# Layer 2 FFN's first slots inside layer 2 attention's tail, one sequence's roots on VectorE, and constant products in layer 0's FFN

## The chip, the cores and the metric

The kernel runs on one core of a Trainium2 chip. The core has five engines that run on their own and meet at semaphores: TensorE (PE: matrix products and transposes; its weight loads are listed as PEld), VectorE (DVE), ScalarE (ACT), GpSimd (POOL) and SyncE (SP, which here only issues DMAs). The metric is the device time of one execution in microseconds; the time before is the median of three, 2713.35 us (2712.96 to 2721.79).

## The reference

Four layers, each FFN, attention, FFN around a residual `x` of 4 sequences x 512 positions x 128 features in float32:

```python
x = x + 0.5 * ffn(layernorm(x));  x = x + attn(layernorm(x));  x = x + 0.5 * ffn(layernorm(x))
```

Two of the FFNs matter here. Layer 0's FFN takes the mean over the positions of a GELU of 1024 input patterns, keeps for each sequence the 128 largest, passes them to 512 process patterns, keeps the 64 largest, weighs 64-wide values by their softmax, passes the sum to 1024 output patterns and keeps the 128 largest of these; the result is one row that is added to all positions of its sequence. So between its wide first products and its last sum, all work is on vectors of a few hundred to a thousand numbers for each sequence.

Layer 2's FFN is a mixture of 8 experts: a router (128 x 8) chooses one expert for each position, and that expert's gated network (128 to 2 x 512, `a * sigmoid(g)`, 512 to 128) is applied to it, with its biases and unscaled. Layer 2's attention, between the two calls of this FFN, attends inside blocks of 32 positions, 16 heads of 8.

## The kernel before

Everything stays in the core's own memory, `x` and the normed copy `y` as 16 tiles of 128 positions (four tiles a sequence), `yT` as features x positions. Python loops unroll the whole program. A scheduler orders each engine's instructions by a planner's costs; what is passed to `tc.keep_in_program_order` (`mm_in_order` L174, `transpose_in_order`, `pin`) keeps the order of the Python text on its engine, everything else may be placed where it is ready. `mm` (L168) and `transpose` are not so held.

**Small work between the big steps.** `chain(b)` collects small steps of sequence `b` (statistics, scaling, transposes, router logits, routing); `tick()` is called many times in each attention loop and runs the steps whose gap of ticks has passed. `leave_normed` puts into such a chain: statistics of `x`, scaling into `y`, `turn` (transposes into `yT`), and, if the next stage routes, `logits`, and after an odd sequence the three parts of `route`: `choose` (softmax over 8 and first maximum), `count` (positions within each expert, the slots' experts `ei`) and `find` (which position goes to which place in which slot, `come`).

**A root.** `inverse_root` (L189) makes `1/sqrt(v + eps)` for a few numbers a partition: a VectorE addition (L197) and a power on POOL (L198). `statistics` (L212) calls it for four tiles. For wider inputs it uses a bit trick and two Newton steps, eight instructions. `scaled_by_act` (L244) then makes `-mean * r` with two POOL instructions and scales on ACT.

**Layer 0's FFN** (`l0_ffn`, run twice). After the wide products, `largest` finds the 128 largest of 1024: 16 rounds of `max` (8 numbers) and `match_replace` on VectorE (L401, L403), a tree of merges (L409), one transpose `pt_l` of the limit (TensorE), comparisons and prefix sums on VectorE, and two products `place` with constant matrices that number the ties. Then come `pp4` (8 products of 512 columns), `pp`, eight rounds of `max` for the 64 largest (L466), softmax, `pt_w`, `pg`, `po0`, `largest` once more, `po1` and `pb`, which spreads the result to all partitions for the update of `x` (L506). The second call is followed by layer 1's FFN, whose attention begins with products of a constant matrix whose result nobody reads (`idle_product`, L179).

**Layer 2's FFN** (`l2_ffn`, run twice, before and after layer 2's attention). The 2048 positions go in two passes of 8 tiles (sequences 0 and 1, then 2 and 3). In a pass the positions are sorted by expert into at most 15 slots of 128 rows, each slot for one expert (`PASS` = 8, `SLOTS` = 15). `logits` has stored the rows in HBM (`yd`). `slot_steps` makes a queue of steps; step n does

- `send(n-2)`: stores a finished slot `o` to `od` in HBM (SP),
- `load(n+5)`: reads the slot's expert from `ei` and loads that expert's weights, 836 KB, into one of five `w` buffers (SP, L1352),
- `fetch(n+4)`: gathers the slot's 128 rows `xg` from HBM (POOL, L1356),
- `to_features(n+1)`: one transpose, copied out by ACT as `xT`,
- `hidden(n)`: 8 products of 128 columns into the banks `pg` and `pa`, four sigmoids on ACT (L1374), four products `hT` on VectorE (L1375),
- `result(n-1)`: 4 products into `po2`, and the bias on VectorE (L1384).

A buffer of `w` comes free when `result` of its slot has added the bias out of it. The second pass begins after the first (`fetch_result` then gathers the first pass's results back from `od`, L1402). In `l2_ffn` the first pass's steps are spread by hand between what is left of the last sequence's chain: `between` says how many steps follow when so many parts of that chain are left.

**Layer 2's attention** (`l2_attn`). A loop over n = -9 to 19, five places in each; tile n's scores are in step n, its exponentials in n+1, the transposes of the weights (`pt_2a`) in n+2, its sums with the values (`po_2a`) in n+3; a sequence's output is made in step 4b+7 (`turn_sums`, `output`). So from n = 16 on nothing new begins. The chain of sequence 1 reaches `find` at n = 14, and the first pass could be routed from there; its first load and gather are in `l2_ffn`, after the loop.

Of the kernel before, what the change touches and what calls it, by code (L numbers as in the profile page):

```python
# [40 lines left out]
PASS = NT // 2  # L41
SLOTS = PASS + 7


# [60 lines left out]
def tile_macaron(ctx, tc, x_in, const_in, vec_in, w0_in, ws_in, ws3_in, w2f_in, w3_in, out):  # L105
# [73 lines left out]
    def idle_product(tag, n):  # L179

        mm_in_order(bank(tag, "idle")[:, :n], onesm, cst[:, :n])

    def bcast(ap, n):

        return ap[:, :, None].to_broadcast([ap.shape[0], ap.shape[1], n])
# [4 lines left out]

    def inverse_root(sb, dst, src, name, op, c, eng=None):


        n = src.shape[-1]
        if n <= TB:
            v = sb.tile([P, n], F32, tag=name, name=name, bufs=2)
            (eng or nc.vector).tensor_scalar(v, src, c, None, op)  # L197
            nc.gpsimd.tensor_tensor(dst, v, minus_half[:, :n], ALU.pow)  # L198
            return
# [5 lines left out]
        for to, a, b in ((yy, -0.703952253, 1.681913895), (dst, -0.50000016, 1.50000048)):  # L205
# [4 lines left out]
            else:  # L210
                eng.tensor_mul(t, t, xx)
                eng.tensor_scalar(t, t, a, b, ALU.mult, ALU.add)  # L212
                eng.tensor_mul(to, t, yy)

    def statistics(src, b, eng=None, pinned=False):

        st = keep.tile([P, TB, 6], F32, tag="ln_st", name="ln_st", bufs=2)
        mv = keep.tile([P, TB, 2], F32, tag="ln_mv", name="ln_mv", bufs=3)
        r = keep.tile([P, TB], F32, tag="ln_r", name="ln_r", bufs=3)
        for t in range(TB):  # L220
            first = nc.vector.bn_stats(st[:, t, :], src[:, b * TB + t, :])
            if pinned and t == 0:
                tc.keep_in_program_order(first)
            nc.vector.bn_aggr(mv[:, t, :], st[:, t, :])
        inverse_root(keep, r, mv[:, :, 1], "ir4", ALU.add, 1e-5, eng)
        return mv, r
# [10 lines left out]

    ordered = {"act": False}

# [4 lines left out]
    def scaled_by_act(dst, src, b, stats):  # L244

        mv, r = stats
        m = keep.tile([P, TB], F32, tag="ln_m", name="ln_m", bufs=3)
        nc.gpsimd.tensor_mul(m, mv[:, :, 0], r)
        nc.gpsimd.tensor_scalar_mul(m, m, -1.0)
        for i in range(TB):  # L250
# [106 lines left out]
    def l0_ffn(tag, chained):  # L357
        with pool(tag) as sb:
# [18 lines left out]
            def by_neuron(row, name):  # L377
# [3 lines left out]
                for c in range(2):  # L381
                    transpose(pt[:, ts(c, P)], row[:, ts(c, P)])
                nc.vector.tensor_copy(
# [11 lines left out]
            def largest(row, vals, r):  # L395
# [3 lines left out]
                for i in range(P // 8):  # L399
                    m8, src = order[:, ts(i, 8)], w if i else row  # L400
                    nc.vector.max(m8, src)  # L401
                    if i < P // 8 - 1:
                        nc.vector.match_replace(w, m8, src, GONE)  # L403
                two = [sb.tile([64, P], F32, tag=f"two{i}", name="two") for i in range(2)]
                larger(two[0], order, 64, 64)
# [9 lines left out]
                pt = bank("t", "pt_l")  # L415
                transpose(pt[:, :B], turned)
                lim = sb.tile([P, B], F32, tag="lim", name="lim")
# [15 lines left out]
                flat = lambda v: v.rearrange("p c b -> p (c b)")  # L433
                mm(place[:, : 8 * B], const("m1"), flat(equal), True, False)
                mm(place[:, : 8 * B], ones, flat(sums[1]), False, True)
                nc.vector.scalar_tensor_tensor(
# [6 lines left out]
            for c in range(2):  # L443
                transpose(pt[:, ts(c, P)], acc[:, c, :, :].rearrange("p q b -> p (q b)"))
            nc.vector.tensor_scalar_mul(ra, pt[:, :256], 1.0 / S)
# [6 lines left out]
            for c in range(8):  # L452
                mm(p4[ts(c % 4, 32), :], kept[0][:, c, :], piw[:, c, :], c < 4, c >= 4)
            pq = sb.tile([P, 512], F32, name="pq4")
            nc.vector.tensor_copy(pq[:, 0:256], p4[:, 0:256])
            nc.vector.tensor_copy(pq[:, 256:512], p4[:, 256:512])
            pp = bank("m", "pp")
            mm(pp[:B, :], selb.rearrange("p (b n) -> p b n", n=P)[:, :, 0], pq)
            pa = sb.tile([B, 512], F32, name="pact")
# [4 lines left out]
            for i in range(KP // 8):  # L464
# [3 lines left out]
                if i == 0:  # L468
                    nc.vector.tensor_scalar_mul(nm, m8[:, 0:1], -1.0)
            ea = sb.tile([B, 512], F32, name="ea")  # L470
            nc.scalar.activation(ea, pa, AF.Exp, bias=nm)
# [6 lines left out]
            for c in range(4):  # L478
                transpose(pt[:, ts(c, B)], pw[:, ts(c, P)])
            pwT = sb.tile([P, 4, B], F32, name="pwT")  # L480
# [3 lines left out]
            for c in range(4):  # L484
                mm(pg[:64, :B], pv[:, c, :], pwT[:, c, :], c == 0, c == 3)
            nc.vector.tensor_copy(agg[:, :B], pg[:64, :B])
# [3 lines left out]
            for q in range(4):  # L490
                mm(po[ts(q, 32), :256], agg, oiw[:64, ts(q, 256)])
            nc.scalar.activation(oa, po[:, :256], AF.Gelu)
# [3 lines left out]
            for c in range(8):  # L496
                mm(po[ts(c % 4, 32), :D], kept[1][:, c, :], op[:, c, :], c < 4, c >= 4)
            o4 = sb.tile([P, D], F32, name="o4")
            nc.vector.tensor_copy(o4, po[:, :D])
            pb = bank("m", "pb")  # L500
            for b in range(B):
                mm(pb[:, ts(b, D)], selb[:, ts(b, P)], o4)

# [748 lines left out]
    yds = [dram.tile([P * PASS, D], F32, name=f"yd{i}") for i in range(2)]  # L1252
    routed, passes = {}, {}

# [11 lines left out]
    def route(k):  # L1266
# [22 lines left out]
        def count():  # L1289
# [13 lines left out]
            nc.vector.tensor_reduce(base, tri, AX.X, ALU.add)  # L1303
            nc.vector.tensor_add(end, base, nf)
            to = sb.tile([P, PASS, 8], F32, tag="to", name="to")
            nc.vector.scalar_tensor_tensor(
# [16 lines left out]
            for t in range(PASS):  # L1323
                nc.vector.tensor_scalar(st["in_place"][:, t, :], const("iota"), place[:, t : t + 1], None, ALU.is_equal)
            past = sb.tile([P, SLOTS, 8], F32, tag="past", name="past")
            nc.vector.tensor_tensor(past, bcast(const("iota")[:, :SLOTS], 8), rows(end, SLOTS), ALU.is_ge)
            es = sb.tile([P, SLOTS], F32, tag="es", name="es")
            nc.vector.tensor_reduce(es, past, AX.X, ALU.add)
            ei = st["ei"] = sb.tile([P, SLOTS], I32, tag=f"ei{k}", name="ei")
            nc.vector.tensor_scalar_min(ei, es, 7.0)  # L1330

# [9 lines left out]

    def slot_steps(sb, k, tags):

        st, yd = passes[k], yds[k]
        ei, come = st["ei"], st["come"]
# [3 lines left out]
        def load(s):  # L1349
            e = nc.values_load(ei[0:1, s : s + 1], engines=[mybir.EngineType.SP], min_val=0, max_val=7)  # L1350
            w[s] = sb.tile([P, W2F.n], F32, tag="w", name="w", bufs=5)
            nc.sync.dma_start(w[s], w2f_in[bass.ds(e, 1), :, :].rearrange("e p n -> (e p) n"))  # L1352

        def fetch(s):
            xg = sb.tile([P, D], F32, tag="xg", name="xg", bufs=4)
            nc.gpsimd.indirect_dma_start(xg, None, yd[:, :], bass.IndirectOffsetOnAxis(ap=come[:, s : s + 1], axis=0))  # L1356
            xT[s] = xg

        def to_features(s):
            pt = bank(tags["t"], "pt_x")  # L1360
            transpose_in_order(pt[:, :P], xT[s])
            xT[s] = sb.tile([P, P], F32, tag="xT", name="xT", bufs=3)
            nc.scalar.copy(xT[s], pt[:, :P])

        def hidden(s):
            pg, pa = bank(tags["g"], "pg2"), bank(tags["a"], "pa2")
            w1, b1 = W2F(w[s], "w1"), W2F(w[s], "b1")
            for half, p in ((1, pg), (0, pa)):
                for c in range(4):
                    mm_in_order(p[:, ts(c, P)], w1[:, ts(4 * half + c, P)], xT[s])  # L1370
            hT[s] = sb.tile([P, 4, P], F32, tag="hT", name="hT", bufs=3)
            for c in range(4):
                sg = sb.tile([P, P], F32, tag="sg", name="sg", bufs=4)
                nc.scalar.activation(sg, pg[:, ts(c, P)], AF.Sigmoid, bias=b1[:, 4 + c : 5 + c])  # L1374
# [3 lines left out]
        def result(s):  # L1378
            po = bank(tags["m"], "po2")
            w2 = W2F(w[s], "w2")  # L1380
            for c in range(4):
                mm_in_order(po[:, :D], hT[s][:, c, :], w2[:, ts(c, D)], c == 0, c == 3)
            o = sb.tile([P, D], F32, tag="o", name="o", bufs=4)
            nc.vector.tensor_add(o, po[:, :D], W2F(w[s], "b2"))  # L1384
# [6 lines left out]
        def step(n):  # L1391
            for part, lag in ((send, 2), (load, -5), (fetch, -4), (to_features, -1), (hidden, 0), (result, 1)):
                if 0 <= n - lag < SLOTS:
                    part(n - lag)

        return deque(lambda n=n: step(n) for n in range(-5, SLOTS + 3))

# [17 lines left out]

    def l2_ffn(tag, early, between, ticks, gap):

        ready.clear()
        own = {"g": "g", "a": "a", "t": "t", "m": "m"}
        with pool(tag) as sb:  # L1420
            with banks(tag + "pa", **early):
                tags = {"g": "e", "a": "e", "t": "m", "m": "m"} if "e" in early else own
                steps = None
                while chains:
# [44 lines left out]

    def l2_attn(v4s):  # L1470
        pin = tc.keep_in_program_order
        with pool("l2a") as sb:
# [128 lines left out]
            for n in range(-9, NT + 4):  # L1601
                for place, (part, lag) in enumerate(stages):
# [6 lines left out]
                    if n >= 0 or place == 0:  # L1609
                        tick()  # L1610


# [362 lines left out]
    with pool("ws") as wp:  # L1975
# [9 lines left out]
        with pool("l2x") as l2x:  # L1985
            with pool("l1x") as xb:
# [8 lines left out]
                l2_ffn("l2f", {"e": 6, "m": 2}, {23: 3, 19: 2, 10: 4, 2: 3, 1: 3}, (5, 8), 4)  # L1995
            with banks("ps2"):
                routed |= {"g": l2x.tile([P, NT, 8], F32, tag="g2f", name="g2f"), "sb": l2x, "gap": 4}
                l2_attn(v4s)
            l2_ffn("l2g", {"a": 2, "g": 2, "t": 2, "m": 2}, {5: 2, 2: 3, 1: 3}, (19, 31), 10)
    with pool("l3r") as rb:  # L2000
# [148 lines left out]
```

## Time and profile before

| | us |
|---|---|
| median of three executions | 2713.35 |
| the profiled execution | 2706.51 |
| its span, first to last instruction | 2704.8 |
| TensorE busy | 2222.7 (82%) |
| VectorE busy | 1780.4 (66%) |
| ScalarE busy | 1293.6 (48%) |
| GpSimd busy | 959.3 (35%) |
| mean granted clock of TensorE | 0.894 |
| layer 0 FFN, narrow part, first and second call | 50 to 125, 308 to 382 |
| layer 1 FFN's last sequence and layer 2 FFN, first call | about 1160 to 1310 |
| layer 2 attention's tail | 1414 to 1440 |
| layer 2 FFN, second call: first pass, second pass | 1440 to 1500, 1500 to 1551 |

The clock is the share of full speed that the chip grants to TensorE: in this trace it is 1.0 or 0.5, and the means over a stretch lie between. A line of a timeline gives the start, the duration, engine, line, operation, output `<-` inputs, shapes and count, and in brackets how long the engine was idle before it and what ended that.

### The profile page before, as it was taken

To read this page: it belongs to the slowest core of one execution; us is meant where nothing else is said; L and a number is where in the kernel's file an instruction comes from. 1 tells how busy PE (TensorE), PEld (TensorE's weight loads), DVE (VectorE), ACT (ScalarE), POOL (GpSimd) and SP (SyncE) were. 2 spreads that over 40 slices of the span, in tenths; PEclk is the share of its full clock that TensorE was granted. 3 is DMA by queue.
4 is the path that set the end of the run, shared out by engine and by line. 5 is a ranking of instruction groups with operands and counts; after the bars stand their busy time and mean duration, and the time that the engine had idled before them with its cause. 6 is when DMAs were issued, how large, how long until landed. Compare 5 with 4: busy or idle time off the path is not lost. (4 is left out here: it accounts for less than half of the span.)

```text
span 2704.8 us, 50539 instructions
## 1 busy us (share of the span) xinstructions
PE 2222.7 (82%) x18934; PEld 1260.1 (47%) x18934; DVE 1780.4 (66%) x4768; ACT 1293.6 (48%) x3145; POOL 959.3 (35%) x1540
## 2 busy tenths in 40 slices
PE   4277539989778998979767868998889999789988
PEld 2145214434334443458557845555533333455555
DVE  3645376777556777555674477778567775877774
ACT  3044314444423544334333447776525555677774
POOL 2013012333222322334322377676310000877661
PEclk8579759998779999889877989999989999899998
DMA  3043010000000000037205811100000000110100
GB/s 144 0 156 96 0 63 1 1 1 1 1 1 1 2 1 5 5 119 246 100 9 191 266 33 23 22 20 21 5 1 1 1 1 5 28 23 21 23 20 12
DMA packets 38412, 113.17 MB, mean 42 GB/s; under 512 B 6872, under 2 KB 14808, under 8 KB 37656
## 3 DMA queue, kind: packets, MB, share of 16 engines
q1 hardware_dynamic: 34792, 100.94, 11.7%
q0 software_dynamic: 2944, 6.04, 1.3%
q8 instruction: 149, 2.44, 0.4%
q10 hardware_dynamic: 432, 2.98, 0.3%
q14 instruction: 95, 0.78, 0.1%
HBM read 79.78 MB, written 15.47 MB: 35 GB/s over the span
## 5 line engine op out<-in xcount | busy, mean ns | idle before, releaser
L845 ACT ACTIVATE PT<-pk_at 128x512 f32<-128x512 f32 (+3 forms) x768 | 335.4, 488 | 401.6 <-PE pq_at L174 255.7
L174 PE MATMUL pk_at<-qx,km 32*128 32x512 f32 (+3 forms) x1536 | 400.8, 555 | 5.8 <-ACT PT L845 2.7
L817 DVE CUSTOM_DVE_ANT_0 s<-pq_at,cst 128x384 f32<-128x384 f32 (+3 forms) x512 | 249.8, 488 | 98.6 <-PE pq_at L174 45.6
L174 PE MATMUL pq_at<-km,qT 32*128 32x128 f32 (+3 forms) x1024 | 277.2, 505 | 19.1 <-DVE nm L817 15.1
L1678 ACT ACTIVATE s<-s,nm,rn 128x128 f32<-128x128 f32 x512 | 245.5, 482 | 3.1 <-DVE nm L1790 2.3
L848 POOL TENSOR_SCALAR_AFFINE_SELECT PT<-PT 128x256 f32<-128x256 f32 x256 | 104.8, 411 | 387.6 <-ACT PT L845 387.6
L174 PEld LDWEIGHTS pk_at<-qx,km 32*128 32x128 f32 x1536 | 147.0, 190 | 153.4 <-issue 92.4
L174 PE MATMUL po_at<-PT,vh 128*32 128x128 f32 (+3 forms) x2432 | 203.6, 392 | 5.1 <-POOL PT L848 5.0
L819 DVE TENSOR_REDUCE nm<-pq_at 128x1 f32<-128x512 f32 x256 | 165.4, 685 | 55.3 <-PE pq_at L174 53.8
L198 POOL TENSOR_TENSOR ln_r<-ir,minus_half 128x4 f32<-128x4 f32 x64 | 66.1, 1035 | 359.6 <-DVE ir L197 358.4
L1739 POOL TENSOR_TENSOR t<-t,t 128x1024 f32<-128x1024 f32 x64 | 151.7, 2370 | 111.5 <-DVE t L1735 111.2
L174 PE MATMUL pq_at<-km,t 32*128 32x512 f32 x512 | 170.8, 661 | 0.7 <-DVE nm L819 0.4
L174 PE MATMUL p_qk<-w,hT 128*128 128x512 f32 x256 | 136.6, 659 | 10.1 <-DVE t L1735 8.7
L1802 POOL TENSOR_TENSOR s<-s,sm 128x1024 f32<-128x1024 f32 x64 | 121.4, 1897 | 51.1 <-DVE sm L1801 43.1
L171 PE MATMUL pt<-ident,s 128*128 128x128 f32 x640 | 92.2, 291 | 51.9 <-POOL s L1802 34.9
L174 PEld LDWEIGHTS pq_at<-km,qT 32*128 32x128 f32 x1024 | 110.4, 191 | 50.7 <-DVE nm L817 30.7
L174 PEld LDWEIGHTS po_at<-PT,vh 128*32 128x32 f32 x2432 | 54.3, 109 | 170.4 <-issue 126.4
L262 ACT COPY yT<-pt_y 128x512 f32<-128x512 f32 x56 | 32.8, 586 | 194.9 <-PE pt_y L171 194.5
L1678 ACT ACTIVATE sq<-p_qk 128x1024 f32<-128x1024 f32 x64 | 65.5, 1024 | 112.1 <-PE p_qk L174 66.8
L1732 DVE TENSOR_TENSOR t<-p_qk,w 128x1024 f32<-128x1024 f32 x64 | 78.2, 1223 | 60.6 <-ACT sq L1678 59.8
L171 PEld LDWEIGHTS pt<-ident,s 128*128 128x128 f32 x640 | 77.6, 149 | 83.7 <-POOL s L1802 46.7
L171 PE MATMUL pt_y<-ident,y 128*128 128x128 f32 x224 | 50.3, 348 | 76.4 <-DVE y L233 61.3
(435 smaller groups left out, 5287.2 us busy)
## 6 DMA issues: line engine op xcount, KB each, us to landing
w<-in_w2f_dram SPq DMA_DIRECT2D x60, 836.0 KB, 5.0
vb<-v SPq DMA_DIRECT2D x112, 128.0 KB, 2.2
skew<-qe SPq DMA_DIRECT2D x16, 512.0 KB, 3.0
rel<-skew SPq DMA_DIRECT2D x64, 128.0 KB, 3.6
w<-in_w_dram SPq DMA_DIRECT2D x1, 4147.0 KB, 12.4
od<-o SPq DMA_DIRECT2D x60, 64.0 KB, 7.0
w<-in_w_dram SPq DMA_DIRECT2D x1, 3200.0 KB
yd<-y SPq DMA_DIRECT2D x8, 256.0 KB, 2.9
```

Source lines behind the costliest of these rows:

```text
L171: return nc.tensor.transpose(dst, src, ident[: src.shape[0], : src.shape[0]])
L174: tc.keep_in_program_order(nc.tensor.matmul(dst, lhsT=lhsT, rhs=rhs, start=start, stop=stop))
L198: nc.gpsimd.tensor_tensor(dst, v, minus_half[:, :n], ALU.pow)
L262: by_order(nc.scalar.copy(yT[:, b, :], pt))
L817: nc.vector.tensor_tensor_reduce(s[:, :nk], pq[:, :nk], causal[:, S - nk :], 1.0, -BIG, ALU.add, ALU.max, to)
L819: nc.vector.tensor_reduce(to, pq, AX.X, ALU.max)
L845: by_order(nc.scalar.activation(PT[:, i, q0:], pk[:, q0:], AF.Exp, scale=SC8))
L848: nc.gpsimd.affine_select(d, d, pattern=[[0, 2], [1, P]], base=0, channel_multiplier=-1, compare_op=ALU.is_ge, fill=0.0)
L1678: tc.keep_in_program_order(nc.scalar.activation(*args, **kw))
L1732: nc.vector.tensor_mul(by_head(t1), by_head(p3), over(tab[:, 0]))
L1739: nc.gpsimd.tensor_add(t1, t1, t2)
L1802: nc.gpsimd.tensor_mul(s, s, bcast(sm, P))
```

## The change

It has four parts.

1. In `l0_ffn`, `warm(gate, n)` makes a product of `onesm` with a small tile (the gate) and then n products of a constant, none of which is read. It is called after the last six rounds of each `largest` and after rounds 4 to 6 of the middle selection, with the round's eight maxima as gate. Two more constant products stand between and behind the two `place` products. All products and transposes of the narrow part are held in program order.
2. `gathering(b)` is true for the last sequence while a routed pass is waiting. Its statistics then take the root in eight VectorE instructions, and `scaled_by_act` makes `-mean * r` in one VectorE instruction; without it VectorE or POOL, then POOL.
3. `count` makes `ei` before the positions' places. `slot_steps` gets its buffer counts and the lead of the loads as arguments, and drops an empty last step and, for a lead of 3, the early ones.
4. For the second call, the first pass's `slot_steps` are made inside the attention as soon as `find` has run, with a lead of 3, three `w` buffers (two of `xT`, `hT`, `sg`, `o`) in a pool of their own. Three steps follow at once, eight more at the (n, place) pairs of `WITH_ATTN`; `l2_ffn` gets the rest (`begun`), and its `between` has one step more. The second pass has a pool with five `w` buffers.

```diff
+WITH_ATTN = {(NT, 4), (NT + 1, 1), (NT + 1, 2), (NT + 1, 4), (NT + 2, 1), (NT + 2, 2), (NT + 2, 4), (NT + 3, 2)}
...
+    def warm(gate, n, tag="s"):
+
+        mm_in_order(bank(tag, "idle")[:, : gate.shape[1]], onesm[: gate.shape[0], :], gate)
+        for _ in range(n):
+            idle_product(tag, S)
...
-    def inverse_root(sb, dst, src, name, op, c, eng=None):
+    def inverse_root(sb, dst, src, name, op, c, eng=None, steps=False):
...
-        if n <= TB:
+        if n <= TB and not steps:
...
+    def gathering(b):
+
+        return bool(passes) and b == B - 1
...
-        inverse_root(keep, r, mv[:, :, 1], "ir4", ALU.add, 1e-5, eng)
+        if gathering(b):
+            inverse_root(keep, r, mv[:, :, 1], "ir4s", ALU.add, 1e-5, None, True)
+        else:
+            inverse_root(keep, r, mv[:, :, 1], "ir4", ALU.add, 1e-5, eng)
...
-        nc.gpsimd.tensor_mul(m, mv[:, :, 0], r)
-        nc.gpsimd.tensor_scalar_mul(m, m, -1.0)
+        if gathering(b):
+            nc.vector.scalar_tensor_tensor(m, mv[:, :, 0], -1.0, r, ALU.mult, ALU.mult)
+        else:
+            nc.gpsimd.tensor_mul(m, mv[:, :, 0], r)
+            nc.gpsimd.tensor_scalar_mul(m, m, -1.0)
...
+                    if i >= P // 8 - 6:
+                        warm(m8, 1)
...
-                transpose(pt[:, :B], turned)
+                transpose_in_order(pt[:, :B], turned)
...
-                mm(place[:, : 8 * B], const("m1"), flat(equal), True, False)
-                mm(place[:, : 8 * B], ones, flat(sums[1]), False, True)
+                mm_in_order(place[:, : 8 * B], const("m1"), flat(equal), True, False)
+                idle_product("s", S)
+                mm_in_order(place[:, : 8 * B], ones, flat(sums[1]), False, True)
+                idle_product("s", S // 2)
...
+                if KP // 8 - 4 <= i < KP // 8 - 1:
+                    warm(m8, 1)
...
-    def slot_steps(sb, k, tags):
+    def slot_steps(sb, k, tags, lead=5, **bufs):
+        bufs = {"w": 5, "xg": 4, "xT": 3, "hT": 3, "sg": 4, "o": 4} | bufs
...
-            for part, lag in ((send, 2), (load, -5), (fetch, -4), (to_features, -1), (hidden, 0), (result, 1)):
+            for part, lag in ((send, 2), (load, -lead), (fetch, -4), (to_features, -1), (hidden, 0), (result, 1)):
...
-        return deque(lambda n=n: step(n) for n in range(-5, SLOTS + 3))
+        return deque(lambda n=n: step(n) for n in range(-max(lead, 4), SLOTS + 2))
...
-    def l2_ffn(tag, early, between, ticks, gap):
+    def l2_ffn(tag, early, between, ticks, gap, begun=None):
...
+                steps = None
+                if begun:
+                    begun["tags"].update(own)
+                    steps = begun["steps"]
...
                     if n >= 0 or place == 0:
                         tick()
+                    slots(n, place)
...
-            l2_ffn("l2g", {"a": 2, "g": 2, "t": 2, "m": 2}, {5: 2, 2: 3, 1: 3}, (19, 31), 10)
+            with pool("l2s") as l2s:
+                begun = {"tags": {"g": "s", "a": "s", "t": "t", "m": "m"}, "steps": None}
+
+                def slots(n, place):
+                    if 0 not in passes:
+                        return
+                    if begun["steps"] is None:
+                        begun["steps"] = slot_steps(l2s, 0, begun["tags"], 3, w=3, xT=2, hT=2, sg=2, o=2)
+                        for _ in range(3):
+                            begun["steps"].popleft()()
+                    if (n, place) in WITH_ATTN:
+                        begun["steps"].popleft()()
+
+                with banks("ps2"):
+                    routed |= {"g": l2x.tile([P, NT, 8], F32, tag="g2f", name="g2f"), "sb": l2x, "gap": 4}
+                    l2_attn(v4s, slots)
+                l2_ffn("l2g", {"a": 2, "g": 2, "t": 2, "m": 2}, {5: 2, 3: 1, 2: 3, 1: 3}, (19, 31), 10, begun)
```

## The prediction

> **What bounds the kernel now.** I read the page's slices first, then the windows table of the stages that the diff touches, then their timelines, the chain of waits and the landings of the weight loads.
>
> ```profile
> PE   4277539989778998979767868998889999789988
> DVE  3645376777556777555674477778567775877774
> PEclk8579759998779999889877989999989999899998
> ```
> A digit is 67.6 us. TensorE leads nearly everywhere, except in slices 2 and 6 (68 to 135 us, 338 to 406 us), layer 0's FFN, and slices 18 to 22, layer 2. The clock row dips in both.
>
> ```profile
> 308.00:382.00 74.00, 14.20 (x74) 7.53 (x74) 54.81 (x198) 4.26 (x5) 0.00 (x0) 0.55 0.03 7
> 330.00:335.00 5.00, 4.11 (x18) 1.01 (x18) 0.58 (x4) 0.00 (x0) 0.00 (x0) 0.50 0.00 0
> 335.00:340.00 5.00, 1.02 (x2) 0.12 (x2) 3.11 (x9) 1.42 (x2) 0.00 (x0) 0.84 0.00 0
> 385.00:390.00 5.00, 4.48 (x7) 1.18 (x6) 4.02 (x26) 0.00 (x0) 4.89 (x4) 0.50 1.06 458
> 390.00:395.00 5.00, 4.58 (x9) 1.80 (x8) 3.83 (x12) 0.59 (x1) 3.52 (x3) 0.67 0.14 60
> ```
> Columns: stretch, its length, busy time of PE, PEld, DVE, ACT, POOL, granted clock, DMA share, GB/s. Layer 0's selection is one serial chain: VectorE 54.8 of 74 us, and TensorE's 14.2 us all on that chain, at half clock. The clock does rise in it: a burst from 331.30 us has it up at 335.3 (0.84 of the next 5 us), after 4.0 us; the constant products from 384.70 us have it up at 393.3, after 8.6 us.
>
> ```profile
> 331.30 3.64 PE L168 MATMUL pp<-w,kept 128*32 128x512 f32 x16 [0.83 <-DVE kept L440]
> 335.90 1.02 PE L168 MATMUL pp<-pq,cst 128*4 128x512 f32 x2 [0.96 <-DVE pq L456]
> 78.43 1.86 PE L168 MATMUL pp<-pq,cst 128*4 128x512 f32 x2 [0.96 <-DVE pq L456]
> ```
> The same product `pp` took 1.86 us in the first call at half clock and 1.02 in the second at full: a ratio of 0.55, my measure of what a higher clock is worth.
>
> ```profile
> 1439.51 0.69 DVE L1587 TENSOR_TENSOR x<-po,x 128x512 f32<-128x512 f32 x1 [3.32 <-PE po L174]
> 1439.68 2.92 SPq L1352 DMA_DIRECT2D w<-in_w2f_dram  x5
> 1441.49 0.17 DVE L197 TENSOR_SCALAR ir<-ln_mv 128x4 f32<-128x4 f32 x1
> 1445.11 1.05 POOL L198 TENSOR_TENSOR ln_r<-ir,minus_half 128x4 f32<-128x4 f32 x1
> 1448.18 0.45 PE L171 MATMUL pt_x<-ident,xg 128*128 128x128 f32 x1 [8.70 <-DMA xg<-yd,come]
> ```
> Layer 2, second call: the weights and rows of the first pass are asked for only after layer 2 attention's last output (1439.5 us), though `come` was known at 1421.3. TensorE waits 8.7 us. Sequence 3's root, ready at 1441.66, starts on POOL at 1445.11, behind four gathers.
>
> ```profile
> 1440.00:1450.00 10.00, 0.97 (x4) 0.71 (x5) 2.71 (x14) 0.28 (x2) 5.92 (x6) 0.50 0.94 274
> 1450.00:1500.00 50.00, 48.68 (x408) 47.38 (x408) 27.32 (x121) 25.56 (x79) 13.16 (x14) 0.95 0.83 276
> 1500.00:1552.00 52.00, 45.63 (x388) 43.62 (x387) 26.56 (x105) 21.91 (x77) 20.80 (x22) 1.00 0.83 270
> ```
> From 1450 us on both the DMA (0.83) and TensorE (48.7 of 50) are near full: the gain can only come from the 9 us before 1450, from the attention's gappy tail, and from the 6.4 us of idle in the second pass.
>
> **Layer 0 FFN, two calls.** No step of VectorE's chain is removed. Added per call: 6 gated products in each of two selections, 3 in the middle one, and two between and behind the `place` products. One gated step is an 8-column product plus a 512-column one. At half clock the latter takes 2.09 us (384.70: 4.18 for two), the former 0.47 (`pl`, 1.88 for four): 2.56; at full clock 1.02 + 0.26 = 1.28 (397.15; `pl` at 1454.89). The first gate opens at 60.7 us (ten rounds of 0.98 us after 50.5, and a `max` of 0.43), so at half clock TensorE is solidly busy. With the clock up R us later the six end at 60.7 + R + (6 - R/2.56) x 1.28 = 68.4 + R/2; `pt_l`, now queued behind them in order, is wanted at 70.1. R = 4.0 (row above) ends at 70.4, R = 8.6 at 72.7. The stretch at 384.70 had gaps and transposes in it, the burst at 331.30 had none, as these have none: I take R = 5, late by 0.8.
>
> What then runs at 0.55 of its time: second `place` 0.64, `pp4` 3.64, `pp` 1.86 (first call only), `pt_w` 0.58 + `pg` 1.02 + `po0` 1.08 behind the middle products, then `place` 0.64, `po1` 1.08, `pb` 2.08. Savings: 0.3 + 1.64 + 0.84 + 1.2 + 0.3 + 0.49 + 0.94 = 5.7 us, 4.9 in the second call; less 2 x 0.8 each: 4.1 + 3.3 = **-7.4**. The product between the `place` pair is free at full clock (1.02 in a gap of 0.77 plus the 0.3 saved); the last one has 0.83 of VectorE over it. The middle three start at 87.6 and end at 91.4 + R/2, before `pt_w` (94.4) unless R is over 6. The pinning of products that were already in this order costs nothing; the chain hides it. Bounds: -10.6 with no lateness, -0.2 with R = 8.6, and, the clock never rising, +32 (below).
>
> Between `pp` (80.3) and the first middle product (87.6) TensorE is idle for 7 us; at 307.5 such a stretch took the clock from 1.00 to 0.50 within 5 us, so the middle products start at half clock, as priced. [...]
>
> **Roots on VectorE, first call.** The new path makes 8 dependent small operations (0.2 us apart, as 1465.57, 1465.77, 1465.97) plus one for the mean: 1.8 us, against 2.0 on POOL when POOL is free (1215.43 to 1217.46), and 1.6 against 1.3 where only the scale follows. Two of the three uses trade evenly. The third doesn't:
>
> ```profile
> 1172.23 0.17 DVE L197 TENSOR_SCALAR ir<-ln_mv 128x4 f32<-128x4 f32 x1
> 1178.29 2.04 POOL L198 TENSOR_TENSOR ln_r<-ir,minus_half 128x4 f32<-128x4 f32 x2
> 1181.13 3.19 ACT L252 ACTIVATE y<-y,ln_m,ln_r 128x128 f32<-128x128 f32 x8 [3.86 <-POOL ln_m L249]
> ```
> POOL stood behind a gather that waits for TensorE, then did both sequences' roots, then ACT both scalings. With sequence 3 off POOL and ACT, sequence 2 needs one root (1.0 less) and four scalings (1.6 less): slot 0's sigmoid and `hT`, for which TensorE sits idle 6 us until 1188.97, come about **-2.4** earlier. Bounds: 0 (something else was as late) and -2.6.
>
> **Layer 2, second call.** Before: three loads and three gathers go out at 1416 to 1425, on queues that stand idle (SP's next was `yd` at 1430.25). Seven `hidden` and six `result` steps go into the order between sequence 2's logits and sequence 3's last sums. A slot costs 2.79 us of TensorE (0.11 + 1.79 + 0.89), one table load of 1.28 on ACT. But the weight ring shrinks from five to three: load n+3 waits for `o` of n, which waits for `hidden` n+1, so two slots take a landing plus 3.1 us (issue 0.12, `hidden` 1.79, `result` 0.89, `o` 0.3). A load alone lands in 4.5 us (median of the 12 between 1190 and 1255), so 3.8 us a slot against 2.79.
>
> I walked the order with these: `hidden` 0 at 1433.5, `o` 0 at 1441.2, `o` 3 at 1452.2, sequence 3's output at 1461.8 instead of 1439.5, its root in 1.8 us and no queue, logits at 1470, routing counted at 1484 (`ei` 1486), `result` 14 at 1492.6, `pi` to 1494.3. The first rows of pass 2 are then fetched in the open (0.5 + 1.0 + about 6, the median landing of `xg` here being 6.1): pass 2 starts at 1502.2, 1.7 later than now (1500.5). Queued behind the waits: on SP the `od` and `yd` stores stand behind a waiting load, up to a slot (nobody reads them before pass 2); on POOL four early gathers (1.25 us each) end at 1426.6, before sequence 2's root of 1428.06. Pass 2's weights, in a ring of their own, are asked for at 1486 and not from 1494 on. Now pass 2 takes 49.8 us for 15 x 2.79 + 0.9 = 42.8 of work; 4.6 of the 7.0 idle is
>
> ```profile
> PE pg L174 <- DMA w<-in_w2f_dram: 4.6, 5, 1.4
> ```
> and goes away; 2.4 stays. End: 1502.2 + 42.8 + 2.4 = 1547.4 against 1550.3, **-2.9**. Each us of landing costs 6 us (12 slots, one landing for two). Bounds: 4.3 (fastest) gives -4; 6.2 (median from 1490 to 1510, DMA full) gives +7; the last of five issued together took 14.8, but never more than three fly here. The earlier `ei` is six small operations, 0.5 us, hidden by the wait for `come`. The dropped empty steps cost nothing.
>
> **Sum.** -7.4 - 2.4 - 2.9 = -12.7. The profiled execution took 2706.5 (span 2704.8), 0.25% under the median of 2713.35, so it gives 2694 and the median 2700.6: I say 2701, its own range 2692 to 2710.
>
> **Rivals.** (B) The tail takes slots better than the walk says and the second pass streams without a stall: the 9 idle us before 1450 and the 4.6 of weight waits are both gained, less 1.7: -12 in place of -2.9, 2691. For it: TensorE idle in 1414 to 1418 and 1438 to 1449. Against: the ring of three. (C) The ring eats it: landings of 6.2 us make layer 2 +7 and the total -2.8, 2711. For it: the DMA's 0.83. Against: at 3.8 us a slot it isn't full. (D) Slower: the gated products don't lift the clock in time. Six at half clock end at 60.7 + 15.4 = 76.1, 6 us after `pt_l` is wanted, four times; between the `place` pair 2.09 don't fit into 0.77 and behind it 1.2 not into 0.83, 1.7 more each time, 0.9 in each middle: 24 + 6.8 + 1.8 = +32, less the other 5.3: 2740. It eats layer 0's gain from R = 8.7 on (4 x (R/2 - 1.7) = 10.6) and the whole change's from R = 11.4. For it: 8.6 at 384.70. Against: 4.0 at 331.30.
>
> **How the numbers follow.** A difference under 0.3%, 8 us, can't be told from no change here. Forecast 0.45, B 0.20, C 0.18, D 0.17. Faster: 0.38 of the forecast, all of B, 0.03 of C: 0.61; same 0.07 + 0.13 + 0.02 = 0.22; slower 0.02 + 0.15 = 0.17. The range 2684 to 2724 holds the forecast, C and most of B, and stops short of D.
>
> **What would show it.** Right: clock near 1.0 at `pp4` (2.0 us, not 3.64) and at `pb` (1.1), `pt_l` less than 1 us late; ACT's scaling near 1174 for sequence 3; weights asked for near 1416, sequence 3's output 20 us later than now, 3.8 us a slot, fewer waits for `w` in the second pass. Wrong: `pt_l` waiting on products at half clock; `w` landing in 6 us or more; the second pass starting after 1508.

## The result, and the profile after

| | before | after |
|---|---|---|
| median of 20 executions each, us | 2715.04 (2708.30 to 2726.65) | 2721.64 (2716.21 to 2731.76) |
| ratio after / before | | 1.0029, 95% interval 1.0017 to 1.0041 |
| profiled execution, its span | 2706.51, 2704.8 | 2721.74, 2719.9 |

The change makes the kernel 0.29% slower, some 8 us, where 2701 us was forecast, 12.7 us below the median of before as it was then known (2713.35). The slices of the page after:

```profile
PE   5576679989679999878767778998889999799988
DVE  3745477776666677555664477777567775877774
PEclk8689879998889999779868879999989999899998
```

A digit is 68.0 us. TensorE is busier in slices 2 and 6 (layer 0's FFN, now 5 and 7) and the clock row no longer falls to 5 there. In slices 18 to 22, layer 2, the digits are no better than before. Where the time went is seen best by matching the same instruction in both traces (a MoE call is a call of layer 2's FFN):

| instruction | before, us | after, us | after less before |
|---|---|---|---|
| layer 0 FFN, `max` of the first call | 56.4 | 57.3 | +0.9 |
| behind the second call, `vh` | 410.8 | 400.3 | -10.5 |
| first MoE call, first `pt_x` | 1174.9 | 1159.8 | -15.1 |
| slot 0's result `po` | 1189.0 | 1171.5 | -17.5 |
| `pe_sum`, 23 us later | 1212.1 | 1199.9 | -12.2 |
| behind that call, `x` | 1326.1 | 1320.1 | -6.0 |
| second MoE call, first pass's `pi` | 1417.7 | 1411.4 | -6.3 |
| second pass, a late `po` | 1548.6 | 1559.9 | +11.3 |

So layer 0 gives 10.5 us, slot 0 of the first MoE call comes 2.4 us earlier as predicted, 11.5 us are then lost inside the same call, and 17.6 in the second call. The rest (-4.6 between 411 and 1175 us, +3.8 behind 1560) lies in code that is the same in both.

**Layer 0.** TensorE's timeline of after; columns: start, us, engine, line, operation, and in brackets the idle time before and what ended it.

```profile
61.67 0.59 PE L175 MATMUL idle<-order,onesm 128*128 128x8 f32 x2 [10.81 <-DVE order L418]
64.25 2.06 PE L175 MATMUL idle<-cst,onesm 128*128 128x512 f32 x2
68.00 1.10 PE L175 MATMUL idle<-cst,onesm 128*128 128x512 f32 x2
71.20 0.22 PE L172 MATMUL pt_l<-ident,turned 4*128 4x4 f32 x1
74.50 1.93 PE L175 MATMUL pp<-w,kept 128*32 128x512 f32 x16 [0.27 <-issue]
77.39 1.02 PE L175 MATMUL pp<-pq,cst 128*4 128x512 f32 x2 [0.96 <-DVE pq L477]
91.34 2.08 PE L175 MATMUL idle<-cst,onesm 128*128 128x512 f32 x2
95.55 1.08 PE L175 MATMUL po<-w,agg 64*32 64x256 f32 x8 [0.34 <-DVE agg L509]
121.54 1.16 PE L175 MATMUL pb<-o,cst 128*128 128x128 f32 x8 [0.40 <-DVE o L522]
```

The constant products go from 2.06 to 1.10 us while the six run, `pp4` takes 1.93 us in place of 3.64, `pp` 1.02 for 1.86 and `pb` 1.16 for 2.08. The middle three stay at 2.08, `pt_w` stands behind the last of them (93.35 us), and `po0` (1.08) is as long as before.

**Layer 2, second call.** The timeline of after:

```profile
1410.82 2.57 SPq L1376 DMA_DIRECT2D w<-in_w2f_dram  x3
1458.61 0.69 DVE L1614 TENSOR_TENSOR x<-po,x 128x512 f32<-128x512 f32 x1 [1.51 <-PE po L175]
1471.20 2.08 PE L175 MATMUL pg<-xT,w 128*128 128x128 f32 x8 [3.71 <-DMA w<-in_w2f_dram]
1472.39 0.23 DVE L1309 TENSOR_TENSOR before<-cum,oh 128x64 f32<-128x64 f32 x1
1477.16 3.63 SPq L1376 DMA_DIRECT2D w<-in_w2f_dram  x2
1481.90 1.13 PE L175 MATMUL pg<-xT,w 128*128 128x128 f32 x8 [2.01 <-DMA w<-in_w2f_dram]
1487.88 0.29 PE L175 MATMUL pos<-cum,ones 128*128 128x8 f32 x2
1490.45 1.71 PE L175 MATMUL pg<-xT,w 128*128 128x128 f32 x8 [1.67 <-DMA w<-in_w2f_dram]
1500.74 0.17 DVE L1360 TENSOR_SCALAR come<-pi 128x15 int32<-128x15 f32 x1 [2.27 <-PE pi L175]
1506.96 0.45 PE L172 MATMUL pt_x<-ident,xg 128*128 128x128 f32 x1 [6.26 <-DMA xg<-yd,come]
```

The weights are asked for early (1410.8) and sequence 3's output is late (1458.6), both as the prediction had it. Then TensorE waits for weights before slots 9, 11 and 13. What the count needs is made on VectorE at 1472.4, but `pos`, the count itself, runs at 1487.9: in TensorE's fixed order it stands behind the rest of slot 9 and slots 10 to 12. Of these 15.5 us TensorE is busy for 13.3, the first 4.8 at half clock, and waits 2.0 for slot 11's weights. In before as many slots stood there, but they ran without a wait, and the count followed its input (1461.8 us) by 3.0 us:

```profile
1464.75 0.29 PE L174 MATMUL pos<-cum,ones 128*128 128x8 f32 x2
```

So, in after, `come` for the second pass is known only at 1500.7, when the first pass is over, and TensorE idles 6.3 us while the rows are fetched.

```profile
1470.00:1480.00 10.00, 8.68 (x50) 8.45 (x50) 4.66 (x21) 3.96 (x11) 0.00 (x0) 0.66 0.39 135
1500.00:1510.00 10.00, 1.83 (x11) 1.47 (x11) 0.37 (x2) 0.44 (x2) 4.71 (x5) 0.55 0.73 229
1510.00:1520.00 10.00, 9.60 (x65) 9.41 (x64) 2.25 (x8) 2.64 (x10) 7.54 (x8) 0.76 0.39 125
```

The windows of after (columns as in the prediction; the granted clock stands third from the end) show a second loss: before had the clock at 1.00 without a break from 1455 to 1553 us, after loses it three times, for 6.8 us behind the wait of 3.7, for 3.4 at 1491, and for 13.6 behind the wait of 6.3.

### The profile page after: what moved, and what is told of

It is laid out like the page before. It is cut to its first block, busy times and chain, and to the rows that moved or that the text cites. A ratio compares the mean times of both kernels' runs of the same rounds, so it can differ in the third digit from the quotient of the medians.

```text
span 2719.9 us, 50840 instructions
## 1 busy us (share of the span) xinstructions
PE 2282.9 (84%) x19070; PEld 1293.4 (48%) x19070; DVE 1787.2 (66%) x4798; ACT 1294.9 (48%) x3145; POOL 953.4 (35%) x1532
## 3 DMA queue, kind: packets, MB, share of 16 engines
q1 hardware_dynamic: 34792, 100.94, 11.5%
## 5 line engine op out<-in xcount | busy, mean ns | idle before, releaser
L175 PE MATMUL pq_at<-km,qT 32*128 32x128 f32 (+3 forms) x1024 | 274.5, 501 | 18.3 <-DVE nm L840 14.4
L175 PE MATMUL p_qk<-w,hT 128*128 128x512 f32 x256 | 142.2, 683 | 11.0 <-DVE t L1763 9.6
L1399 DVE SCALAR_TENSOR_TENSOR hT<-pa,w,sg 128x128 f32<-128x128 f32 x240 | 70.8, 344 | 87.8 <-ACT sg L1398 39.7
L1380 POOL DMA_INDIRECT xg<-yd,come x60 | 58.0, 966 | 180.6 <-PE pt_x L172 91.7
L1760 DVE TENSOR_TENSOR t<-p_qk,w 128x1024 f32<-128x1024 f32 x64 | 78.3, 1223 | 61.6 <-ACT sq L1706 57.3
```

Source lines behind the costliest of these rows:

```text
L175: tc.keep_in_program_order(nc.tensor.matmul(dst, lhsT=lhsT, rhs=rhs, start=start, stop=stop))
L1399: nc.vector.scalar_tensor_tensor(hT[s][:, c, :], pa[:, ts(c, P)], b1[:, c : c + 1], sg, ALU.add, ALU.mult)
L1760: nc.vector.tensor_mul(by_head(t1), by_head(p3), over(tab[:, 0]))
```

## The experiments

Times are ratios to before, measured on the same chip in the same job; 0.001 is 2.7 us. In the second call I read milestones in us from the moment the first pass's `come` is made (1421.3 us in before, 1415.0 in after); "count" is the last `pos`, "end" the last slot's bias on VectorE. Each row is one profiled execution, so it can differ from the ratio by some us.

| kernel | slot 0 | seq. 3 out | logits | count | last `o` of pass 1 | pass 2 begins | end |
|---|---|---|---|---|---|---|---|
| the prediction's walk | 12.2 | 40.5 | 48.7 | 62.7 | 71.3 | 80.9 | 126.1 |
| before | 28.4 | 18.2 | 34.4 | 44.0 | 78.2 | 79.2 | 129.0 |
| after | 14.3 | 43.6 | 52.0 | 73.3 | 85.8 | 94.5 | 146.5 |
| e1, layer 0 only | 27.7 | 18.3 | 33.4 | 43.0 | 77.9 | 79.0 | 127.5 |
| e4, no roots | 12.1 | 41.1 | 49.7 | 70.8 | 81.6 | 94.1 | 141.6 |
| e6, early count | 12.1 | 41.2 | 49.8 | 63.0 | 82.7 | 83.8 | 133.2 |
| e7, ring of three alone | 23.1 | 18.2 | 29.1 | 42.2 | 100.3 | 101.4 | 149.5 |
| e8, three loads early | 19.5 | 18.4 | 29.7 | 39.3 | 72.1 | 73.1 | 121.4 |

### The parts alone

e1 is before with the hunks of `l0_ffn` and `warm`; e2 is before with `gathering`, `inverse_root`'s new path and their two uses; e3 is before with the rest of the diff; e4 is after with

```diff
-        return bool(passes) and b == B - 1
+        return False
```

> Before plus layer 0's gated products alone. If the clock's gain there is real and passed on to the end (theory): 10.5 us faster, ratio 0.996, as the trace of after had 5.6 us gained by the end of layer 0's first call and 4.9 more by the end of its second. If what is gained is given back behind it (rival: the clock's windows only fall elsewhere): within 3 us of before.

Measured: 0.9968 (0.9954 to 0.9981), 8.7 us faster. The gain is real and is passed on.

> Before plus the last sequence's roots on VectorE alone. Prediction's step: 2.4 us faster, from the first call of layer 2's FFN. What the trace of after suggests: slot 0's products 2 to 4 us earlier, then all of it lost by the end of that call and some 7 us more, because the clock falls in the second pass there (0.75 and 0.84 over 25 us where before had 1.00): 5 to 9 us slower. Rival: that clock fall is chance of the profiled execution; then within 2 us of before.

Measured: 1.0016 (1.0006 to 1.0026), 4.3 us slower: it is a loss, just under the 5 to 9 us that the trace of after suggested. The fall of the clock in the second pass, given there as the cause, is not in its profile. TensorE's timeline in the first MoE call, before and then with the roots alone:

```profile
1188.98 2.08 PE L174 MATMUL po<-w,hT 128*128 128x128 f32 x8 [5.97 <-DVE hT L1375]
1192.58 1.99 PE L174 MATMUL pe<-ws,yT 128*128 128x512 f32 x4 [0.67 <-ACT yT L262]
1194.41 0.95 PE L174 MATMUL pl<-ws,yT 128*128 128x8 f32 x8
```

```profile
1186.31 2.08 PE L174 MATMUL po<-w,hT 128*128 128x128 f32 x8 [3.91 <-DVE hT L1385]
1189.92 3.78 PE L174 MATMUL pe<-ws,yT 128*128 128x512 f32 x4 [0.68 <-ACT yT L272]
1193.49 1.71 PE L174 MATMUL pl<-ws,yT 128*128 128x8 f32 x8
```

And the window behind it, with the roots alone:

```profile
1186.00:1198.00 12.00, 11.01 (x38) 8.33 (x39) 5.06 (x25) 3.46 (x7) 2.09 (x2) 0.50 0.31 99
```

Slot 0's result comes 2.67 us earlier. But the products behind it run at half clock throughout (0.50 over 12 us), 3.78 us for `pe` in place of 1.99. By the clock record it fell at 1185.2 and rose at 1192.0 in before, 6.8 us; here it fell at 1184.7 and rose at 1198.3, 13.6 us. At 1209 us TensorE is 2.3 us behind before.

> Before plus the slots in layer 2 attention alone. Theory: the ring of three and the late count of the last sequences make the second call 17 us longer, as in the trace of after: 17 us slower, ratio 1.006. Rival: a part of that is the roots' (they change the order on VectorE in the same place); then 8 us slower or less. Prediction's step was 2.9 us faster.

Measured: 1.0045 (1.0029 to 1.0060), 12.2 us slower. In its profile the second call loses 13.8 us (from 3.6 us ahead of before to 10.2 behind). The loss is the slots' own; the 17 of the first trace is above it.

> After with the roots left where before has them. If roots are neutral and the slots cost 17: as after, 6 to 8 us slower than before. If the roots cost 5 to 9 us: within 3 us of before. If the second call's loss is the roots': 8 us faster than before.

Measured: 1.0014 (1.0003 to 1.0024), 3.8 us slower: between the first two cases, as e1 and e3 together have it. The three parts alone add up, -0.0032 + 0.0016 + 0.0045 = 0.0029, to the whole change's 1.0029.

### Why the roots lose

e5 is e2 with constant products that fill the wait, e12 is before with five of them and no roots:

```diff
         def result(s):
+            if s == 0 and tags["g"] == "e":
+                held = bank("e", "idle")
+                for _ in range(3):
+                    mm_in_order(held[:, :S], onesm, cst[:, :S])
             po = bank(tags["m"], "po2")
```

> The roots alone (as in the run before) plus three 512-column products whose result nobody reads, on TensorE, ahead of slot 0's result in the first call of layer 2's FFN. Theory: the roots do bring slot 0's result 2.7 us earlier, but TensorE then restarts at half clock and the clock comes back one or two windows later (13.6 us down in place of 6.8), which costs 3 to 4 us; with the gap filled the clock stays up, so the gain stays and the products behind it run at full clock: 3 to 5 us faster than before, 7 or so faster than the roots alone. Rival: the roots' loss is VectorE's own (nine small operations in front of others); then still 2 to 4 us slower than before.

Measured: 0.9993 (0.9982 to 1.0003): not the gain of 3 to 5 us, but 0.0023 (6 us) better than the roots alone. The profile shows the mechanism at its place:

```profile
1179.16 2.74 PE L174 MATMUL idle<-cst,onesm 128*128 128x512 f32 x6
1183.11 1.26 PE L174 MATMUL po<-w,hT 128*128 128x128 f32 x8 [1.22 <-DVE hT L1385]
1185.49 1.99 PE L174 MATMUL pe<-ws,yT 128*128 128x512 f32 x4 [0.67 <-ACT yT L272]
```

The clock stays up from 1178.3 to 1222.7 us, `pe` takes 1.99 again, and against before TensorE goes from 3.4 us ahead at `pt_x` to 7.4 ahead at 1189 us: 4.0 us gained and kept, as expected there. VectorE's nine small operations are the same in both, so they aren't the loss. That the whole kernel gained less is not explained by this place; in its profile the second call is 4 us longer than in before.

> Before plus five constant products ahead of slot 0's result in the first call of layer 2's FFN, and no roots. If TensorE's clock is what the roots lost, it stays up here too: slot 0's result at the same place as in before, and the products behind it 1.5 us shorter in the profile, 0.9994 of before; the roots' own 2.7 us are then the rest of the 4 us that roots and constant products gained together. If the constant products delay slot 0's result (five at half clock are 10.4 us, the gap is 6): 4 us slower at that place.

Measured: 0.9999 (0.9987 to 1.0010). The clock stays up, but only 0.5 us is gained at the place (expected 1.5; `pl` now waits 0.8 us for VectorE). So the other 3.5 of the 4 us need the roots.

The clock record agrees over the fourteen profiled executions. Without roots and filling (before, e1, e3, e4, e6, e7, e8, e10) the clock is down 6.8 us at this place in all eight; with roots and no filling (after, e2) 13.6 us in both; with filling (e5, e9, e11, e12) it doesn't fall. In the gaps of 5.97 and 3.91 us above the clock fell, 2.2 and 2.3 us after their start; in the one of 1.22 us it did not. But in after it fell behind one of 1.67 us too (slot 13's wait, at 1490.8) and stayed up behind one of 2.01 (slot 11's, which ended at 1481.9), and in e12 it stayed up behind one of 1.66, so in these traces the length of the gap is not what decides.

What decides is not shown. In before the clock was up 3.0 us after TensorE had started again (1188.98 to 1192.0), with the roots alone 12.0 us after it (1186.3 to 1198.3), though TensorE was busy for 11.01 of the 12 us from 1186 to 1198; 1.71 us of this went to `pl`, whose products have 8 columns. So the longer fall comes with the roots (two kernels against eight) and goes with the filling (four); why a start 2.7 us earlier makes it longer stays open, and no run varied the work behind the gap by itself.

After's first MoE call has lost 5.9 of its 11.5 us by 1253 us (17.5 ahead at slot 0's result, 11.6 there); the longer fall lies in this part. The other 5.6 lie at the start of its second pass (11.6 us ahead at 1253 us, 6.0 at 1297), where the clock fell twice (for 6.8 us at 1248.5, for 3.4 at 1262.1). It falls there in after, e1, e8, e9 and e12 and not in the nine others, with and without roots, so it is not the roots' doing. Why it falls with one kernel's slots and not with another's stays open.

### Why the slots lose

e6 is e4 with another table of slots between the last sequence's steps:

```diff
-                l2_ffn("l2g", ..., {5: 2, 3: 1, 2: 3, 1: 3}, (19, 31), 10, begun)
+                l2_ffn("l2g", ..., {5: 2, 3: 1, 2: 1, 1: 1}, (19, 31), 10, begun)
```

> After without the roots, and with one slot in place of three between the last sequence's choice of expert and its count, and one in place of three between its count and its search; the slots taken away follow behind. Theory: the count stands behind three slots that wait for weights, 8 to 16 us after it could be made, and nothing is left to run while the second pass's first rows are fetched; two slots (4.4 us each) ahead of the count less and four left behind the search: come 9 to 15 us earlier, 7 to 10 us faster than the kernel without the roots (which was 1.0014 of before), so 0.998 to 0.999 of before. Rival: only the ring of three sets the pace; then the last result of the first pass and the start of the second stay where they are and the time is within 3 us of that kernel's.

Measured: 0.9971 (0.9959 to 0.9983), 0.0043 or 11.6 us better than e4. The timeline:

```profile
1457.00 2.08 PE L175 MATMUL pg<-xT,w 128*128 128x128 f32 x8 [3.67 <-DMA w<-in_w2f_dram]
1465.46 0.34 PE L175 MATMUL pos<-cum,ones 128*128 128x8 f32 x2
1473.92 0.16 DVE L1360 TENSOR_SCALAR come<-pi 128x15 int32<-128x15 f32 x1
...
1486.93 1.16 PE L175 MATMUL pg<-xT,w 128*128 128x128 f32 x8 [0.25 <-ACT xT L1387]
```

The count runs as soon as it can, `come` is known 13 us before the second pass begins, and its first slot waits 0.25 us for nothing but a copy. The first pass's last result is where it was (82.7 against 81.6 in e4), the second pass begins 10.3 us earlier. So the rival falls: it is the order behind the last sequence, not the ring, that makes e4 slower than layer 0's part alone. But e6 is no better than e1: the early slots gain nothing either. e7 says why. It is e1 with the ring of three in a pool of its own, loads three slots ahead, and `count` making `ei` early as in after:

```diff
-            w[s] = sb.tile([P, W2F.n], F32, tag="w", name="w", bufs=bufs["w"])
+            if three:
+                w[s] = three.tile([P, W2F.n], F32, tag="w", name="w", bufs=3)
...
-                        steps = slot_steps(sb, 0, tags)
+                        steps = slot_steps(sb, 0, tags, 3, begun) if begun else slot_steps(sb, 0, tags)
```

> Before with layer 0's products, and with a ring of three weight buffers in place of five in the first pass of the second call, nothing of it started early. Layer 0's products alone were 0.9968 of before. By the slots of after (4.3 to 4.6 us each while they wait for weights, 2.8 in before) the first pass grows by 10 to 15 us and the time is 0.9968 + 0.004 to 0.005 = 1.001 to 1.002. Rival: with the DMA nearly full anyway (0.83) two more buffers are worth little: within 3 us of the kernel with layer 0's products alone.

Measured: 1.0024 (1.0011 to 1.0038), 0.0056 or 15 us worse than e1 (10 to 20 by the two intervals). Not everything of it starts late: its pool is free during the attention, so three loads go out at 1403.2 us, and slot 0 begins 4.6 us earlier than in e1. The waits of TensorE in that call (line, for what, us in total, times, longest):

```profile
PE pg L175 <- DMA w<-in_w2f_dram: 22.4, 10, 4.8
```

The prediction showed 4.6 us over 5 waits in before. With three buffers the fifteen slots take 71.7 us from the first `hidden` to the last, 5.1 each, against 3.3 in before. So the ring of three costs about 15 us in spite of its early loads. e6 has the same ring, with gathers and slots in the attention and its own table, and is 0.0053 or 14 us faster than e7: what the early slots bring and what the ring costs are about equal, and they cancel.

e8 keeps the early loads and drops the rest: three loads and four gathers inside the attention, no slot there, and for slots 3 and up the five buffers of `l2_ffn`'s own pool, which are free once the attention is over.

```diff
+            early = late is not None and s < lead
+            w[s] = home(early).tile([P, W2F.n], F32, tag="w", name="w", bufs=lead if early else 5)
...
+                if late is not None and part is load and n >= 0:
+                    which = {0: [3, 4, 5], 1: [6], 2: [7]}.get(n, [n + 5])
...
-WITH_ATTN = {(NT, 4), (NT + 1, 1), (NT + 1, 2), (NT + 1, 4), (NT + 2, 1), (NT + 2, 2), (NT + 2, 4), (NT + 3, 2)}
+WITH_ATTN = {(NT + 2, 4)}
```

> Layer 0's products, and of the slots only the first three loads and four gathers inside layer 2 attention (no hidden or result step); the first pass starts behind the attention's last output as in before, with slots 3 and up in the five buffers of before. If the wait for the first weights and rows (8.7 us in before) was the one thing to be gained and the ring and the late output of the last sequence took it away: 6 to 9 us faster than layer 0's products alone, 0.9935 to 0.9945 of before. Rival: the DMA's rate sets both passes from there on (0.83 to 1.0), and the start of the first pass is worth nothing: as layer 0's products alone, 0.9968.

Measured: 0.9933 (0.9917 to 0.9950), 18 us faster than before and 0.0035 or 9.5 us better than e1.

```profile
1426.34 0.69 DVE L1621 TENSOR_TENSOR x<-po,x 128x512 f32<-128x512 f32 x1 [3.40 <-PE po L175]
1426.83 2.22 SPq L1378 DMA_DIRECT2D w<-in_w2f_dram  x4
1427.36 1.92 PE L175 MATMUL pg<-xT,w 128*128 128x128 f32 x8
1437.88 1.06 PE L175 MATMUL pg<-xT,w 128*128 128x128 f32 x8
```

Slot 0 begins 1.0 us after the attention's last output, where before waited 8.7, the loads of slots 3 and up go out meanwhile, and the call ends 6.1 us earlier than in e1.

e10 adds to e8 slots 0 and 1 inside the attention's tail (`WITH_ATTN = {(NT, 4), (NT + 1, 4), (NT + 2, 4)}`, loads 3 to 7 in step 2).

> The kernel with three loads early (0.9933 of before) with slots 0 and 1 begun inside layer 2 attention's last tiles, the rest behind, in the five buffers. If slots in the tail fill time in which TensorE is idle: two slots of 2.8 us gained, 3 to 5 us less, 0.992 of before. If they delay the last sequence's output, and its choice, count and search set the second pass: its output 6 us later, and 0.993 to 0.995.

Measured: 0.9938 (0.9925 to 0.9952), as e8. The last sequence's output comes 4.8 us later (23.2 us behind `come`, 18.4 in e8), and the end with it (125.2 against 121.4): time in the tail is not free, it is taken from the chain that the second pass waits for.

### Together

e9 is e8 with the roots and the three constant products, e11 is after with the constant products and e6's table.

> The kernel with three loads early (0.9933 of before) plus the roots on VectorE plus the three constant products ahead of slot 0's result in the first call. Theory: with TensorE's clock held the roots keep their 2.7 us and the products behind them run at full clock, 4 us as in the profile of the roots with constant products; in the second call the roots are worth nothing. So 4 us less: 0.9918 of before. Rival: the roots cost VectorE something in the second call that eats it (there the last sequence's choice ended 4 us later in that profile): 0.993 to 0.994.

Measured: 0.9897 (0.9883 to 0.9911), 28 us faster than before. Its profile gains 3.3 us on e8's in the first MoE call, as expected, and is 3.4 shorter in the end; by time it is 0.0036 better, more than that, and the two intervals don't settle how much more.

> After, with two edits: the slots between the last sequence's choice, count and search cut to one each (as in the run on the count), and the three constant products in the first call. By those runs (0.9971 for after without the roots with the early count; roots with constant products 0.9993 of before): 0.9964 of before, against 1.0029 for after. If the count's gain and the clock's are the same microseconds: 0.998 or more.

Measured: 0.9951 (0.9936 to 0.9966), a little better than the 0.9964 expected: two edits, a table and three products, turn the change from 0.29% slower into 0.49% faster.

## Why the prediction was wrong

**Layer 0: right, with one wrong part.** Predicted -7.4, measured -8.7 (-5.1 to -12.4). The clock came up 5.8, 3.9, 6.9 and 4.4 us after the first gated product (61.67 to 67.5, 107.9 to 111.8, 313.2 to 320.1, 360.0 to 364.4), 5.3 in the mean where 5 was taken. `pt_l` was some 0.2 us late in the first call, 0.7 in the second. What failed is the middle selection: 2.4 us were booked there (1.2 a call), and over the nine profiled kernels with this part the middle three products brought the clock up in 1 of 18 cases. At half clock they end after `pt_w` is wanted: in after they cost 0.8 us a call. What the work behind the last sums gained in after, 2.5 and 3.2 us with the clock higher there, was not booked and made it up, so that the sum came out is luck. The bound of -0.2 for R = 8.6 leaves out 1.3 us a call by which the middle products would be late; it should have been +2.4. The rival of 2740, in which the gated products don't lift the clock in time, did not occur: the six lifted it in all 36 cases.

**Roots: the step was right, what follows it was not asked.** "Come about -2.4 earlier" was 2.67. The prediction saw "TensorE sits idle 6 us" and took the gain as passed on; its bounds, 0 to -2.6, excluded a loss, and the measured part is +4.3 (+1.6 to +7.0). It had read for layer 0 what a gap does to the clock (1.00 to 0.50 within 5 us at 307.5) and did not ask it here.

**Layer 2, second call: the step that failed is "routing counted at 1484".** Predicted -2.9, bounds -4 to +7; measured +12.2 (+7.8 to +16.2) for the part alone. Up to the logits the walk holds within 3.3 us (table above). Then it lets the count run when its inputs are ready; in after it waited 15.5 us in TensorE's order behind the rest of slot 9 and three more slots, run late and in part at half clock. That moved the count by 10.6 us, the second pass by 13.6 and the end by 20.4. Cutting those slots to one gave back 11.6 us (e6). The prediction had asked what is queued behind the waits on SP and on POOL, and left out TensorE, whose order the change writes by hand.

**Its sizes.** 3.8 us a slot was taken from a lone landing of 4.5 us; the first seven slots took 4.0, all of them 4.7 with the stall before slot 9, for which two loads were in flight and the weights came 6.5 us after the issue (1464.7 to 1471.2). The second pass was to take 45.2 us; it took 52.0 in after (47.5 in e4), where it begins at half clock with rows and weights still on the way; what each of these is worth was not taken apart. The rival "the ring eats it" (2711) named a loss that is there, about 15 us (e7) where it had 10 (7 less the -2.9), but not the one that made the change slower: of the 15.1 us by which this part missed its -2.9, the order of the count is 11.6.

**The sum.** Forecast -12.7, the three parts measured together +7.8: layer 0 missed by -1.3, the roots by +6.7, the slots by +15.1. The chances put 0.17 on slower; the one slower rival sat in layer 0. The two parts that lost had bounds that were too narrow, for one reason: each was walked on the engines that the edit touches, and what came next was TensorE's: its clock behind the roots, its order in front of the count.

## What to carry to other kernels

A step that is moved earlier takes its work away from where it was cover: before pulling slots forward, ask which chain they were hiding (here choice, count, search and first gather of the last sequence) and keep some behind its last link. Pull forward what needs only a queue and a buffer (loads, gathers) and leave the arithmetic; here that was worth 9.5 us more than layer 0's part, and arithmetic in the tail nothing more. And where a wait in front of TensorE is shortened but not removed, check the clock behind it, and fill the wait: a gain of 2.7 us became a loss until three products of 0.9 us held the clock.

## What the runs showed of the hardware

- At slot 0 of the first MoE call the clock was down for 6.8 us in the eight kernels without roots and filling, for 13.6 in the two with roots and no filling, and not at all in the four with filling. With the roots alone TensorE had started again 2.7 us earlier than in before (1186.31 against 1188.98).
- Being busy alone did not lift the clock. In the middle selection TensorE is busy by the trace for 7.6 us on end (85.8 to 93.4 us in after), and the clock stayed at 0.50 (17 of 18 cases); in `largest` it came up after 3.6 to 6.9 us of much the same products (36 of 36). There the 512-column products fill 2.06 of every 2.13 us (64.25 to 66.38), in the middle 2.08 of 2.53 (88.82 to 91.34), the rest being a product with a gate of 4 rows. Which of these differences decides is not shown.
